# Nine of 49 blocks of a graph layer summed from gathered rows instead of packed slots

## The chip, the cores and the metric

The kernel runs on one core of one Trainium2 chip. The metric is the device time of one execution in microseconds, as the median of several runs; the profile is of one more execution and gives the span from the core's first to its last instruction. Five engines work side by side, each through its own fixed list of instructions: TensorE (PE, with weight loads as PEld), VectorE (DVE), ScalarE (ACT), GpSimd (POOL) and the sync engine (SP), whose list here holds DMA issues. An instruction may wait for semaphores; everything behind it in the same list then waits too.

## What is computed

One relational graph layer with a residual and a layer norm, on 6,250 nodes of 128 features and 100,000 edges that are sorted by destination:

```python
Xs = X[src]
m_data = Xs @ W_data.T + b_data
m_ctrl = Xs @ W_control.T + b_control
msg = jnp.where((edge_types == 0)[:, None], m_data, m_ctrl)
agg = jax.ops.segment_sum(msg, dst, num_segments=X.shape[0])
out = jax.nn.relu(agg + (X @ W_self.T + b_self))
x = layernorm(x + out)
```

Every edge takes the row of its source node under one of two linear maps and adds it to its destination node. All of it is float32; the kernel carries each float32 value as three bfloat16 parts that sum to it, which is why rows have 384 columns.

## The kernel before

**Lead-in (0 to about 100 us).** `load_x` and `split_x` bring x in, transposed, in seven parts and split it in three bfloat16 parts (`x3`). `multiply` forms both linear maps for all 49 blocks of 128 nodes (49 x 2 = 98 sub-tables, `NT`) with nine matmuls a block and a bias matmul; `take` and `leave` split the results in three parts again. They stay in SBUF as `m3`, and `store` also writes them to a table in DRAM. `store_x` writes the split x to DRAM (`x3_t`).

**Edges.** The destinations are cut into 49 blocks of 128 nodes. Since edges are sorted, the edges of a block lie in one window of 2,304 edges (`WIN`, 18 rows of 128, `KT`). `starts` finds where each window begins and loads it.

**Packing (per group of five blocks, `GROUPS`).** The rows of `m3` are already on the chip, so a block's messages are not fetched one by one. For each block, the up to 32 edges (`R`) of each of the 98 sub-tables get slots: `bucket_hots` and `ranks` (matmuls into `acc`, reductions into `slot`) number the edges of each sub-table, `fill_a` and `fill_b` (matmuls into `small`) put the source row and the destination of each slot into place, `fill_c` writes the slots to DRAM (`packed`) and handles edges that found no slot: it fetches up to 32 such rows with an indirect DMA from the table (`msg_s`).

**The main loop (per block).** `spread` reads the block's slots back to all partitions (`rows`, 784 KB), `select` makes them one-hot on VectorE. Then 25 tiles (`NS`) follow. A tile covers four sub-tables of 32 slots: `gather` multiplies four one-hots of 32 columns by the rows of `m3` into a PSUM tile `g_ps`, `evict` copies it to SBUF as `gs` on ScalarE, and `add_up` multiplies it by the one-hot of destinations (`hot_d`) into `agg`, in four column matmuls. `own_of` adds the node's own map (12 matmuls on x read from `x3_t`, `load_own`), and the last tile adds the leftover rows and the bias. `finish_blocks` and `normalise` do the rest on VectorE and ScalarE, and the result is stored a group at a time.

**The order.** All these are generators whose steps name a cost by engine, the steps they need and a due time. A planner (`Order.run`) places the steps while the kernel is built: among those that can start within `CLOSE` of the earliest it takes the one due first. The result is a fixed order on each engine. `BLOCK` is the planned time of a block, `BUILT` the planned end of the lead-in. When the program runs, only semaphores hold the engines to each other.

**Buffers.** PSUM has eight banks: three of `ps_a` (`small`, `acc`, `agg`; one each) and five of `ps_g` (`GB`). `row_pool` holds `RB` blocks of rows, `EB` = 8 tiles of `gs`.

Of the kernel before, what the change touches and what calls it, by code (L numbers as in the profile page):

```python
# [19 lines left out]
P = 128  # L20
# [12 lines left out]

GROUPS = (4,) + (5,) * 9
Q = max(GROUPS)
NPG = len(GROUPS)
STARTS = [sum(GROUPS[:i]) for i in range(NPG)]
R = 32
NS = (NT + 3) // 4
NC = 4 * NS  # L40
RB = 4
M = 8
SLOT = 128.0
PARTS = (4, 8, 8, 8, 8, 8, 5)
KC = 6
DC = 13
# [3 lines left out]
class Order:  # L50
# [9 lines left out]
    AFTER = 0.25  # L60
    CLOSE = 0.2

# [38 lines left out]
def kernel(  # L101
# [24 lines left out]


    nc = tc.nc
    dram = ctx.enter_context(tc.tile_pool(name="dram", bufs=1, space=DRAM))
    const = ctx.enter_context(tc.tile_pool(name="const", bufs=1))  # L130
    table = dram.tile([NT * P, D3], BF16, name="table")
    x3_t = dram.tile([NB, D, 3 * P], BF16, name="x3_t")
    packed = dram.tile([NB, NT * R], BF16, name="packed")
    total = const.tile([1, 1], I32, name="total")
# [69 lines left out]
def sums_over_windows(ctx, tc, x, xt, edges, w, bias, table, x3_t, packed, total,  # L204
# [3 lines left out]
    const = ctx.enter_context(tc.tile_pool(name="consts", bufs=1))  # L208
    work = ctx.enter_context(tc.tile_pool(name="work", bufs=2))
    row_pool = ctx.enter_context(tc.tile_pool(name="row_pool", bufs=RB))  # L210
    ps_a = ctx.enter_context(tc.tile_pool(name="ps_a", bufs=1, space=PSUM))
# [30 lines left out]
    counted = {}  # L242
    for n in sorted({DC, *GROUPS}):
        counted[n] = const.tile([P, P, n], BF16, name=f"count{n}")
        G.iota(counted[n], pattern=[[1, P], [0, n]], base=0, channel_multiplier=0,
               allow_small_or_imprecise_dtypes=True)
# [34 lines left out]
    def three_parts(parts, whole, left):  # L281
# [17 lines left out]
    spill_tiles = [(const.tile([P, Q * P], BF16, name=f"hot_s{i}"),  # L299
                    const.tile([P, D3], BF16, name=f"msg_s{i}")) for i in range(2)]  # L300
    slot_values = [const.tile([P, (Q + 1) // 2, NC], BF16, name=f"vs{i}") for i in range(2)]
    slot_b = {n: const.tile([P, R, n], BF16, name=f"slot{n}") for n in sorted({*GROUPS})}

    def constants():
# [23 lines left out]

        for hot, msg in spill_tiles:
            V.memset(hot, 0.0)  # L330
            V.memset(hot[R : R + 1, :], 1.0)
            V.memset(msg, 0.0)
            V.tensor_copy(msg[R : R + 1, :].rearrange("p (i c) -> p i c", i=3),
                          parts[0:1, :, 2 * D :])

    win = {}
    first = const.tile([1, NB], I32, name="first")
    counts = const.tile([P, NPG], F32, name="counts")
    m3 = const.tile([P, NT, D3], BF16, name="m3")
    m3v = m3.rearrange("p (t b) c -> p t b c", t=2)  # L340

    def starts():
# [12 lines left out]
        V.tensor_scalar_min(first, first_ps[:1, :NB], float(E - WIN))  # L355
        for b in range(NB):
            grp = [g for g in range(NPG) if STARTS[g] <= b][-1]
            yield step(("win", b), {"S": 0.84}, "first", *([("fields", grp - 2)] if grp > 1 else []),
                       lag=2.0)
            if b == STARTS[grp]:  # L360
                win[grp] = work.tile([P, Q, KT, 3], I32, name="win")
            at = nc.values_load(
                first[0:1, b : b + 1], engines=(SP,), min_val=0, max_val=E - WIN,
                skip_runtime_bounds_check_because="it counts edges and is held to E - WIN",
            )
            nc.sync.dma_start(
                win[grp][:, b - STARTS[grp], :, :],
                edges[ds(at, WIN), :].rearrange("(p k) c -> p k c", p=P),
            )
# [8 lines left out]
    LEAD, BUILT = 12.0, 85  # L378
    BLOCK = 13.5
    AHEAD = 12.0  # L380

    def due(kind, *i):
        if kind in ("p", "g") and i[0] in ("root", "rooted", "scale", "apply", "out"):
            n = i[1] + 1
            return BUILT + 10 + BLOCK * sum(GROUPS[:n])
        if kind in ("counted", "turned", "first"):
# [13 lines left out]
        if kind in ("win", "xs", "agg", "o", "whole", "sum"):  # L400
            b = i[0]
            begun = BUILT + BLOCK * b
            if kind == "win":
                return begun - 2 * BLOCK * GROUPS[1] - 20
            return begun + {"whole": BLOCK + 0.5, "sum": BLOCK + 3}.get(kind, 0.3 * BLOCK)
        if kind in ("rows", "sel", "d", "g", "e", "s"):
            of = {"rows": 1, "sel": 1, "d": 2}.get(kind, NS)
            lead = {"rows": -9, "sel": -3, "d": -1, "g": 0, "e": 1, "s": 2}[kind]
            return BUILT + BLOCK * (i[0] + (i[1] / of if len(i) > 1 else 0)) + lead
        n = GROUPS[i[0]]  # L410
        end = BUILT + BLOCK * STARTS[i[0]] - AHEAD
# [14 lines left out]
    def load_x():  # L426
        for g, n in enumerate(PARTS):
            yield step(("xt", g), {"A": 0.45}, *([("x3", g - 3)] if g > 2 else []), lag=4.0)
            xts[g] = build.tile([D, max(PARTS), P], F32, name="xt", bufs=3)[:, :n]
            A.dma_start(xts[g].rearrange("p b c -> p (b c)"),  # L430
                        xt[:, at_part[g] * P : (at_part[g] + n) * P])
# [21 lines left out]
    def multiply():  # L453
        for i, (g, b, n) in enumerate(two_blocks):
            free = [("yl", two_blocks[i - YB][1])] if i >= YB else ["biased"]
            yield step(("y", b), {"T": 1.08 * n}, ("x3", g), *free)
            ys[b] = y = ps_y.tile([P, 2, 2 * D], F32, name="y")
            for j in range(n):
                for i in range(3):
                    for k in range(3):  # L460
                        T.matmul(y[:, j, :], x3s[g][:, b + j - at_part[g], i, :],  # L461
                                 w3[:, k, : 2 * D], start=i == j == k == 0, stop=False,
                                 skip_group_check=True)
                T.matmul(y[:, j, :], ones_b, bias3, start=False, stop=True, skip_group_check=True)  # L464

# [242 lines left out]
    d_hots, g_tiles, gs_tiles, aggs, xss, x3b, hs_, mvs = {}, {}, {}, {}, {}, {}, {}, {}  # L708
    XS = 4
    DB, EB, GB = 4, 8, 5  # L710

# [9 lines left out]
    def select():  # L721

        for b in range(NB):
            yield step(("sel", b), {"V": 1.2}, ("rows", b))
            V.tensor_scalar(rows[b], rows[b], pid1, None, op0=ALU.is_equal)  # L725

    def to_hots():
        tiles = [(b, c) for b in range(NB) for c in range(-(-NS // DC))]
        for i, (b, c) in enumerate(tiles):
# [12 lines left out]

    tiles = [(b, g) for b in range(NB) for g in range(NS)]

# [10 lines left out]
    def evict():  # L755
        for i, (b, g) in enumerate(tiles):
            free = [("s", *tiles[i - EB])] if i >= EB else []
            e = yield step(("e", b, g), {"A": 0.37}, ("g", b, g), *free)
            gs_tiles[b, g] = gs = late.tile([P, D3], BF16, name="gs", bufs=EB)
# [15 lines left out]

    def load_own(name, blocks):
        for i, b in enumerate(blocks):
            free = [("sum", blocks[i - XS])] if i >= XS else []
            yield step(("xs", b), {"S": 0.9}, ("rows", b), "built", *free, lag=4.0)
            x3b[b] = late.tile([D, 3, P], BF16, name=f"x3_{name}", bufs=XS)  # L780
            nc.sync.dma_start(x3b[b].rearrange("p i c -> p (i c)"), x3_t[b])
            xss[b] = load_rows(b, late, f"xs_{name}", XS)

    def own_of(blocks, begun):

        for i, b in enumerate(blocks):
            yield step(("agg", b), {"S": 0.0}, *([("whole", blocks[i - 1])] if i else []))
            yield step(("o", b), {"T": 0.5}, ("xs", b), begun(b))
            for i in range(3):
                by_columns(aggs[b].rearrange("p (i c) -> p i c", i=3), x3b[b][:, i, :],  # L790
                           w3[:, :, 2 * D :], start=False, stop=False, skip_group_check=True)

    def finish_blocks():
        for b, (grp, q) in enumerate(blocks):
# [3 lines left out]
            if q == 0:  # L798
                hs_[grp] = late.tile([P, Q, D], F32, name="h_p")
                mvs[grp] = work.tile([P, Q, 2], F32, name="mv_p")  # L800
# [16 lines left out]


    late = ps_g = None

    def close_build():
        nonlocal late, ps_g
        yield step("built", {"S": 0.0}, "stores", ("yl", NB - 1), *[("x3_t", g) for g in range(len(PARTS))])
        early.close()
# [9 lines left out]
        take(1, "ym", "y1"), leave(1, "y2", "ym"), take(2, "yl", "y2"), constants(), store_x(), store(), close_build(),  # L834
        load_own("p", list(range(NB))), own_of(list(range(NB)), lambda b: ("s", b, 0)),
    ], due)


    total_ps = ps_a.tile([P, 512], F32, name="small")
    T.matmul(total_ps[:1, :NPG], ones[:, 0:1], counts, start=True, stop=True)  # L840
    total_f = work.tile([1, 1], F32, name="total_f")
    V.tensor_reduce(total_f, total_ps[:1, :NPG], axis=AX.X, op=ALU.add)
    V.tensor_copy(total, total_f)
# [121 lines left out]
```

## Time and profile before

| what | value |
|---|---|
| median of 3 runs | 721.98 us (721.96 to 722.43) |
| span of the profiled execution | 717.1 us, mean granted TensorE clock 0.990 |
| matmuls | 14,698 |
| evictions `gs` on ScalarE | 1,225, 489.5 us busy |
| indirect DMAs on GpSimd | 11 |
| bytes moved by DMA | 73.05 MB, 102 GB/s over the span |

Busy shares tell how long an engine had something in hand. TensorE's matmuls overlap: each is listed with its whole duration, while four column matmuls run beside each other, so a busy count near 100% tells that there were no pauses and not what a matmul costs; that is read from the starts of successive matmuls in the timeline. In a waits or timeline line, the bracket names how long the engine was idle before the instruction and who released it. GpSimd is almost unused: it makes some constants at the start and issues the indirect DMAs.

### The profile page before, as it was taken

What the parts mean: (1) busy time and instruction counts of PE and PEld (TensorE: products, weight loads), DVE (VectorE), ACT (ScalarE), POOL (GpSimd) and SP (SyncE); (2) the same over time, 40 slices, a digit from 0 to 9 for tenths busy, and PEclk for the clock granted to TensorE, in tenths of its full rate; (3) what the DMA queues carried; (4) which work ended last, traced back from release to release, by engine and by line L of the source; (5) the groups of instructions that cost most, each with busy time, mean ns of one, the idle gap of its engine ahead of it and who ended that gap; (6) DMA issues with size and microseconds to landing.
All of it is one profiled execution on the core that took longest, in us unless ns stands there. A gap on an engine that the chain in (4) does not pass through costs nothing.

```text
span 717.1 us, 33878 instructions
## 1 busy us (share of the span) xinstructions
PE 667.4 (93%) x14698; PEld 574.3 (80%) x14698; DVE 527.5 (74%) x1101; ACT 572.6 (80%) x1407; POOL 23.3 (3%) x21
## 2 busy tenths in 40 slices
PE   3799979999999999999989989999999999999993
PEld 2667747898898888889878888998988897887882
DVE  8565568788869958886985888699689778657321
ACT  3666546889789887888978888898889888798994
POOL 4000000000000000000000000000000000001000
PEclk9999989999999999999999999999999999999997
DMA  5566564053006105301710530160062026006200
GB/s 162 163 209 217 165 212 155 9 170 124 11 15 243 52 3 193 108 8 45 222 42 4 202 97 9 42 235 24 4 222 76 4 92 201 7 4 222 75 4 23
DMA packets 57564, 73.05 MB, mean 102 GB/s; under 512 B 12292, under 2 KB 50191, under 8 KB 57359
## 3 DMA queue, kind: packets, MB, share of 16 engines
q1 hardware_dynamic: 55806, 66.70, 28.6%
q10 hardware_dynamic: 1154, 3.41, 1.5%
q8 instruction: 116, 1.90, 1.1%
q0 software_dynamic: 448, 0.72, 0.3%
q14 instruction: 40, 0.33, 0.2%
HBM read 52.85 MB, written 17.96 MB: 99 GB/s over the span
## 4 chain that ended last, share of the span: by engine, by line
PE 57%; DVE 24%; DMA 10%; ACT 3%; issue 3%; SPq 1%; DVEq 0%; ACTq 0%
PE agg L220 21%; PE g_ps L752 17%; PE acc L220 7%; PE small L603 5%; DVE slot L565 4%; DMA x_p<-x_t 4%; DMA out<-h_p 4%; PE y L461 4%; DVE hot_d L739 4%; DVE hot_st L548 3%; DVE two L586 3%; ACT h_p L179 2%; DVE rows L725 1%; DVE hr L581 1%; PE y L480 1%
## 5 line engine op out<-in xcount | busy, mean ns | idle before, releaser
L760 ACT CAST gs<-g_ps 128x384 bf16<-128x384 f32 x1225 | 489.5, 514 | 67.9 <-PE g_ps L752 61.5
L220 PE MATMUL agg<-gs,hot_d 128*32 128x384 bf16 x4900 | 407.1, 332 | 2.8 <-ACT gs L760 1.9
L752 PE MATMUL g_ps<-m,rows 128*32 128x384 bf16 x4900 | 399.9, 328 | 3.1 <-DVE rows L725 2.8
L220 PEld LDWEIGHTS <-hot_d 128*32 128x32 bf16 x4900 | 232.5, 137 | 28.4 <-issue 5.9
L752 PEld LDWEIGHTS <-rows 128*32 128x32 bf16 x4900 | 217.0, 137 | 22.6 <-issue 5.6
L565 DVE TENSOR_REDUCE slot<-acc 128x5 bf16<-128x490 f32 (+1 forms) x180 | 117.5, 653 | 78.7 <-PE acc L220 76.1
L739 DVE TENSOR_TENSOR hot_d<-count,to 128x1664 bf16<-128x1664 bf16 x98 | 104.6, 1068 | 11.4 <-PE agg L220 9.1
L220 PE MATMUL acc<-hot_st,rest 128*32 128x490 bf16 (+1 forms) x680 | 72.8, 375 | 13.7 <-DVE slot L565 13.2
L220 PE MATMUL acc<-hot_st,tri 128*32 128x490 bf16 (+1 forms) x720 | 77.7, 370 | 1.3 <-DVE hot_st L548 1.3
L548 DVE TENSOR_TENSOR hot_st<-count,st_b 128x2940 bf16<-128x2940 bf16 (+1 forms) x30 | 58.8, 1964 | 16.0 <-PE small L603 8.1
L473 ACT CAST m<-y 128x512 bf16<-128x512 f32 (+1 forms) x75 | 40.5, 580 | 31.7 <-PE y L464 23.8
L603 PE MATMUL small<-hot_st,two 128*32 128x98 bf16 x1764 | 64.9, 291 | 0.0
L461 PE MATMUL y<-w,x 128*128 128x256 bf16 x441 | 57.8, 279 | 6.1 <-DVE w L283 3.2
L603 PEld LDWEIGHTS <-two 128*32 128x32 bf16 x1764 | 60.4, 118 | 0.9 <-issue 0.2
L220 PEld LDWEIGHTS <-rest 128*32 128x32 bf16 x680 | 30.5, 96 | 34.1 <-issue 30.3
L461 PEld LDWEIGHTS <-x 128*128 128x128 bf16 x441 | 43.7, 100 | 13.3 <-issue 3.2
L725 DVE TENSOR_SCALAR rows<-rows,pid 128x3136 bf16<-128x3136 bf16 x49 | 50.2, 1024 | 4.0 <-DMA rows<-packed 3.9
L142 DVE TENSOR_REDUCE whole<-agg 128x128 f32<-128x384 f32 x49 | 27.1, 553 | 34.6 <-PE agg L220 33.3
L220 PE MATMUL agg<-w,x_p 128*32 128x384 bf16 x588 | 36.4, 327 | 4.0 <-DMA x_p<-x_t 3.6
L693 POOL DMA_INDIRECT msg_s<-table,row_i x10 | 14.7, 1475 | 630.1 <-PE g_ps L752 484.6
L220 PEld LDWEIGHTS <-x_p 128*32 128x32 bf16 x588 | 20.7, 97 | 9.2 <-DMA x_p<-x_t 5.4
L220 PEld LDWEIGHTS <-tri 128*32 128x32 bf16 x720 | 24.5, 97 | 2.8 <-issue 2.1
(123 smaller groups left out, 369.5 us busy)
## 6 DMA issues: line engine op xcount, KB each, us to landing
rows<-packed SPq DMA_DIRECT2D x49, 784.0 KB, 6.7
table<-m SPq DMA_DIRECT2D x10, 768.0 KB, 4.2
x_p<-x_t SPq DMA_DIRECT2D x49, 96.0 KB, 7.1
x_t<-x SPq DMA_DIRECT2D x5, 768.0 KB, 7.7
xs_p<-in_x SPq DMA_DIRECT2D x49, 64.0 KB, 6.5
xt<-in_xt ACTq DMA_DIRECT2D x5, 512.0 KB, 4.4
out<-h_p SPq DMA_DIRECT2D x8, 320.0 KB, 3.9
win<-in_edges SPq DMA_DIRECT2D x49, 27.0 KB, 1.9
```

The source lines that it names most:

```text
L142: nc.vector.tensor_reduce(whole, agg.rearrange("p (i c) -> p c i", i=3), axis=AX.X, op=ALU.add)
L220: T.matmul(out[c : c + 32], lhsT[:, c : c + 32], rhs, **flags)
L461: T.matmul(y[:, j, :], x3s[g][:, b + j - at_part[g], i, :], w3[:, k, : 2 * D], start=i == j == k == 0, stop=False, skip_group_check=True)
L473: A.copy(part_of(b, n, i), ys[b][:, :n, :].rearrange("p b (t c) -> p t b c", t=2))
L548: V.tensor_tensor(hot, counted[n][:, None, 1 : NT + 1, :].to_broadcast([P, KC, NT, n]), fields[grp][2][:, c * KC : c * KC + KC, None, :].t ...
L565: V.tensor_reduce(slots[grp][:, k, :], by_q, axis=AX.X, op=ALU.max)
L586: V.tensor_tensor(two[:, :, i], hr, f[:, ks, None, :].to_broadcast(wide), op=ALU.mult)
L603: T.matmul(vt[c0 : c0 + R, q // 2, :], two[:, k, i, :, q], hot[:, k, :, q], start=c == k == 0 and q < 2, stop=c * KC + k == KT - 1, skip_g ...
L725: V.tensor_scalar(rows[b], rows[b], pid1, None, op0=ALU.is_equal)
L739: V.tensor_tensor(hot, counted[DC][:, :, :n], places[grp][:, q, None, c * DC : c * DC + n].to_broadcast([P, P, n]), op=ALU.is_equal)
L752: T.matmul(g_ps[t * R : (t + 1) * R, :D3], rows[b][:, :, s], m3[:, s, :], start=True, stop=True)
L760: (A.copy if e == "A" else V.tensor_copy)(gs, g_tiles.pop((b, g))[:, :D3])
```

## The change

Nine of the 49 blocks are taken out of the packing. Their edges' rows are fetched directly: GpSimd issues one indirect DMA for each of the 18 rows of 128 edges of a window, 162 in all, each of which brings 128 rows of 384 bfloat16 (768 bytes) from the table in DRAM to 128 partitions. A one-hot of destinations (`hot_g`, VectorE, six of them in one instruction) then sums them with four column matmuls. No slots, no gather matmuls and no eviction are needed for these blocks. It is meant to hand work from TensorE, ScalarE and VectorE to the idle GpSimd and to the DMA queues. The 40 other blocks stay packed in eight groups of five. The gathered blocks get due times that spread them over the whole run (`PACE` = 3.2 us for each gather), so that a gathered quad of matmuls comes up between packed ones all the time.

The other parts:
- The own x of a block is loaded as soon as its part of `x3_t` is stored, into a pool of its own that exists from the start (before: only once the lead-in's buffers were closed).
- In `multiply` the bias matmuls of a pair of blocks stand behind both blocks' products, and the step waits for `bias` and no longer for `biased`.
- In the last packed group the planner may give evictions to VectorE; in the built order it gives it 15 of 125.
- To make room: four `g_ps` tiles (`GB`) instead of five, three blocks of rows (`RB`) instead of four, two `xt` buffers instead of three. The gathered sums take a PSUM bank of their own (`agg_g`), the gathered rows three buffers (`MB`), their one-hots two (`XB`).
- `BLOCK` 13.5 to 13.2, `CLOSE` 0.2 to 0.1. The windows of the nine blocks are loaded right behind those of the first two groups.

```diff
-GROUPS = (4,) + (5,) * 9
+GROUPS = (5,) * 8
...
-RB = 4
+XS = 4
+RB = 3
...
-    CLOSE = 0.2
+    CLOSE = 0.1
...
+    hot_b = const.tile([P, P], BF16, name="hot_b")
+    msg_b = const.tile([P, D3], BF16, name="msg_b")
...
-        for b in range(NB):
-            grp = [g for g in range(NPG) if STARTS[g] <= b][-1]
+        for b in [*range(STARTS[2]), *range(NPB, NB), *range(STARTS[2], NPB)]:
+            grp = [g for g in range(NPG) if STARTS[g] <= b][-1] if b < NPB else NPG
...
-    BLOCK = 13.5
+    BLOCK = 13.2
+    PACE = 3.2
...
+        if kind in ("gh", "gm", "msg"):
+            k = i[1] * CH if kind == "gh" else i[1]
+            return BUILT + PACE * (i[0] * KT + k) + {"msg": 0, "gh": 2, "gm": 5}[kind]
...
-            xts[g] = build.tile([D, max(PARTS), P], F32, name="xt", bufs=3)[:, :n]
+            xts[g] = build.tile([D, max(PARTS), P], F32, name="xt")[:, :n]
...
-            free = [("yl", two_blocks[i - YB][1])] if i >= YB else ["biased"]
+            free = [("yl", two_blocks[i - YB][1])] if i >= YB else ["bias"]
...
+            for j in range(n):
                 T.matmul(y[:, j, :], ones_b, bias3, start=False, stop=True, skip_group_check=True)
...
-    DB, EB, GB = 4, 8, 5
+    DB, EB, GB = 4, 8, 4
...
-            e = yield step(("e", b, g), {"A": 0.37}, ("g", b, g), *free)
+            costs = {"A": 0.37, "V": 0.53} if b >= STARTS[-1] else {"A": 0.37}
+            e = yield step(("e", b, g), costs, ("g", b, g), *free)
...
-            yield step(("xs", b), {"S": 0.9}, ("rows", b), "built", *free, lag=4.0)
+            yield step(("xs", b), {"S": 0.9}, ("x3_t", part), *free, lag=4.0)
...
+    def gather_rows():
+        for i, (j, k) in enumerate(gathered):
+            free = [("gm", *gathered[i - MB])] if i >= MB else [*stored, "built", "idx"]
+            yield step(("msg", j, k), {"G": PACE}, *free, lag=3.0 - PACE)
+            msgs[j, k] = late.tile([P, D3], BF16, name="msg", bufs=MB)
+            G.indirect_dma_start(
+                out=msgs[j, k], out_offset=None, in_=table[:, :],
+                in_offset=bass.IndirectOffsetOnAxis(ap=idx[:, j, k : k + 1], axis=0),
+            )
...
+    def gathered_sums():
+        for j, k in gathered:
+            free = [("agg", NPB + j)] if k == 0 else [("o", NPB + j)] if k == KT - 1 else []
+            yield step(("gm", j, k), {"T": 0.165}, ("msg", j, k), ("gh", j, k // CH), *free)
+            if k == 0:
+                aggs[NPB + j] = ps_a.tile([P, D3], F32, name="agg_g")
+            by_columns(aggs[NPB + j], g_hots[j, k // CH][:, :, k % CH], msgs.pop((j, k)),
+                       start=k == 0, stop=k == KT - 1, skip_group_check=True)
```

## The prediction

> **What bounds the kernel now.** I read the page's busy shares first, then a table of busy time by stage, then TensorE's timeline, GpSimd's timeline and the DMA landings.
>
> ```profile
> PE 667.4 (93%) x14698; PEld 574.3 (80%) x14698; DVE 527.5 (74%) x1101; ACT 572.6 (80%) x1407; POOL 23.3 (3%) x21
> ...
> core 0: us, PE busy (x) PEld busy (x) DVE busy (x) ACT busy (x) POOL busy (x), PEclk, DMA share, GB/s
> 95.00:126.00 31.00, 25.48 (x488) 17.85 (x489) 23.60 (x60) 17.15 (x43) 0.87 (x1) 0.89 0.64 212
> 438.00:498.00 60.00, 59.19 (x1428) 52.74 (x1424) 49.68 (x105) 52.27 (x133) 1.70 (x1) 1.00 0.26 90
> 650.00:705.00 55.00, 53.44 (x1148) 43.22 (x1144) 21.98 (x50) 53.58 (x140) 2.77 (x1) 1.00 0.25 86
> ```
>
> From about 106 to 650 us TensorE is busy nearly all the time (59.2 of 60 us); ScalarE and VectorE have slack (52 and 50), GpSimd does nothing. From 650 on, with no more buckets to fill, ScalarE is full instead (53.6 of 55). Busy counts overlapping matmuls, so I take TensorE's real price from the timeline:
>
> ```profile
> 115.60 0.34 PE L752 MATMUL g_ps<-m,rows 128*32 128x384 bf16 x4
> 115.76 0.34 PE L220 MATMUL agg<-gs,hot_d 128*32 128x384 bf16 x4
> 115.92 0.34 PE L752 MATMUL g_ps<-m,rows 128*32 128x384 bf16 x4
> ...
> 676.07 1.21 PE L752 MATMUL g_ps<-m,rows 128*32 128x384 bf16 x20
> ...
> 685.83 1.22 PE L752 MATMUL g_ps<-m,rows 128*32 128x384 bf16 x20
> ```
>
> Columns: start, duration, what. Four column matmuls start every 0.162 us though each lasts 0.34: 0.0405 us apiece. The same mark recurs 9.76 us later in the last blocks; that is 25 evictions at 0.39 us, ScalarE's pace.
>
> The new load falls on GpSimd, so I read its few indirect DMAs (32 rows each, the first 49) and the landings:
>
> ```profile
> 8.34 1.13 POOL L275 DMA_INDIRECT er<-in_edges,row_i  x1 [0.20 <-issue]
> ...
> 218.01 1.70 POOL L693 DMA_INDIRECT msg_s<-table,row_i  x1 [61.23 <-PE g_ps L752]
> 278.66 0.87 POOL L693 DMA_INDIRECT msg_s<-table,row_i  x1 [58.95 <-PE g_ps L752]
> ...
> 651.58 2.77 POOL L693 DMA_INDIRECT msg_s<-table,row_i  x1 [61.27 <-PE g_ps L752]
> ...
> 218.58 1.01 DVE L725 TENSOR_SCALAR rows<-rows,pid 128x3136 bf16<-128x3136 bf16 x1
> ...
> rows<-packed SPq DMA_DIRECT2D x49, 784.0 KB, 6.7
> ...
> msg_s<-table,row_i POOLq DMA_INDIRECT x10, 6.5
> ```
>
> The undisturbed one takes 0.87 us. The one at 218.01 meets the selection of rows on VectorE (218.58 to 219.59) and ends at 219.71, just after it. Landing is 6.5 us at the median, 2.7 at the least.
>
> **What the skill says.** (1) "SBUF — State Buffer", section "Who interferes with whom": GpSimd and VectorE share a port pair under an exclusive lock; a VectorE instruction in a two-port mode, or with two SBUF inputs against a GpSimd read, blocks the other fully. The trace agrees: 0.87 becomes 1.70 and 2.77. (2) "DMA: Bandwidth & Descriptors", section "Anatomy of one DMA — SWDGE (gpsimd) path": generation is "small, variable", and the fixed cost of some 2 us is completion. Ten gathers of 32 rows and one of 49 cannot show the slope up to 128. (3) "TensorEngine Tiling (Array Packing)", section "PSUM Bottleneck": after a tiled TensorE the PSUM copy may bound, so both ScalarE and VectorE should evict. The window 650 to 705 shows it.
>
> **The change, part by part.**
>
> *TensorE.* Nine blocks fewer packed: 9 x 200 = 1,800 gather and sum matmuls x 0.0405 = 72.9 us. Two groups of ranks fewer (program order: 1,400 down to 1,120 matmuls into acc, four per 0.21 us): 280 x 0.052 = 14.6. Bucket matmuls 1,764 to 1,440, at 64.9 us / 1,764 = 0.037: 12.0. Small ones, about 1. Added: 9 x 18 x 4 = 648 matmuls on gathered rows x 0.0405 = 26.2. The own-feature and bias matmuls of a gathered block (12 and 4) equal the 12 and 4 it had. Net -74.3.
>
> *ScalarE and VectorE.* ScalarE loses 225 evictions (489.5 / 1,225 = 0.40 each), 90 us. VectorE loses 9 selections, 18 one-hots, 36 slot reductions, 6 bucket one-hots and their fills (1.02, 1.07, 0.65, 1.96, 2.1): about 76 us; it gains 27 one-hots of 768 elements (by size, 768/1,664 x 1.07 = 0.5) and 15 evictions (bounded by the PSUM reduction of the same 384 columns, 0.55): 22 us. Both stay under TensorE, so this is worth nothing by itself until the tail.
>
> *Tail.* ScalarE keeps 110 of the last 125 evictions: 8.6 us a block instead of 9.76. TensorE needs 216 x 0.0405 = 8.75 for the block plus about three gathered quads, 9.3, and now binds. The quads' 0.5 us were counted above, so -(9.76 + 0.5 - 9.3) x 5 = -5.
>
> *Lead-in.* The own matmuls of block 0 waited 1.6 us for x at 113 to 115 us; the early load removes that. But the first gathered quad stands some 4 us of TensorE work behind the first block's first tile (105.8 us before), and its gather may go only when the last table stores (issued at 101.3) have landed, so about 108; in the burst of row broadcasts there it lands 6.5 later. All packed matmuls stand behind that quad: about 5 us in place of 1.6, +3. Bias matmuls last and the wait for the bias hide in TensorE's lead-in, which runs on without a gap from 50 us: 0. Extra loads of edge windows on the DMA queue: 0, before TensorE's queue drains.
>
> *The new wait.* A gathered quad is in TensorE's fixed order; if its message is late, everything behind it stops, then ScalarE and VectorE. Three message buffers: gather k waits for quad k-3. In the built order 73 matmuls lie between quads, and by the prices above 9.1 us of TensorE work lie from quad k-3 to quad k (8.1 at the fifth percentile). In that time GpSimd must issue and the data land. GpSimd's time for 128 rows is not in the trace. Lower end: 0.87, were rows free. Slope from 32 to 49 rows: (1.13 - 0.87)/17 = 15 ns a row, hence 0.87 + 96 x 0.015 = 2.4. Upper end: proportional, 4 x 0.87 = 3.5. I take up to 2.4, as the 49-row one also ran beside VectorE, plus 0.45 for the lock: the VectorE work that blocked it, or has two inputs of that kind, fills about 40% of the time (hot_d 104.6, hot_st 58.8, rows 50.2 and the fills some 63 us of 717), and a meeting cost 0.83 to 1.9. Together 2.9. That is under the 3.2 us at which the quads come (9.1 / 3 and stalls). Landing was 6.5 in bursts with the 32-row issue included; with 2 us more, about 8.5 against 9.1. So it holds, barely, in bursts (DMA share 0.26 of the time): I charge +8, from 0 to 40.
>
> *End.* The last four quads close TensorE's order back to back and the very last gather waits for the fourth from last: issue 2.4 and landing some 1.5: +4. Four PSUM tiles instead of five for gather results, three row buffers instead of four: at most a few us, taken as +2.
>
> Sum: 717.1 - 74.3 - 5 + 3 + 8 + 4 + 2 = 654.8 of span. The metric stands 4.9 above the span (722.0 against 717.1), which gives 659.7. From the other side: a steady group costs 61.5 us, with 1.125 gathered blocks of (72 + 16) x 0.0405 = 3.6 it costs 65.5, so 13.1 a packed block: 106 us of lead-in, 35 x 13.1, 5 x 9.3, and 25 for the slow start (95 to 126 has 5.5 us idle and a lower clock) and the last outputs: 636 of span, 641. I take 653, above the middle of 641 and 660, since stalls have a floor and no ceiling.
>
> **Rivals.**
> A: *Messages come late.* In bursts the loop of three buffers needs 0.2 + 2.9 + 7.5 = 10.6 us per three quads instead of 9.7; over all 54 rounds 572 us, from 108 to 680, and 20 for end and metric: 700. For it: 6.5 us landings for a quarter of the size. Against: only about a quarter to a third of the run has the queues full.
> B: *GpSimd becomes the bound and the kernel is slower.* At 3.5 us proportional and 0.45 for the lock: 162 x 3.95 = 640; 108 + 640 + 17 = 765. The crossing with the old time lies at (722 - 125)/162 = 3.7 us a gather. For it: 2.77 us already seen for 32 rows. Against: 49 rows cost 1.13, far from proportional.
> C: *ScalarE paces it and TensorE's saving is lost.* Its load falls from 53.3 to about 54 per 65.5 us: it does not bind before the tail.
>
> **How the numbers follow.** Forecast (634 to 680): 0.65. A (680 to 720): 0.21. B: 0.12. Within 0.2%: 0.01, C included; the rest lies below 634. Faster is forecast, low rest and A: 0.87. The range begins at 634 (the 641, with some of the 68 us that TensorE's 649 us of pure work leaves idle now closed by the quads) and reaches to 712, which takes in most of A and leaves B out: some 0.83 in all.
>
> **What would show it.** Right: the 162 indirect DMAs of 128 rows average under 3.2 us on GpSimd; TensorE at 9 tenths in all middle slices; its idle time before the gathered quads under 20 us in total; 13.1 us a packed block; the tail at about 9.3. Wrong: GpSimd busy near 80% or more with each gather near 4 us; TensorE's idle time before quads of 50 us or more, released by DMA; the saving of matmuls there but in gaps.

## The result and the profile after

| | before | after |
|---|---|---|
| median | 721.97 us | 689.91 us (688.36 to 690.45) |
| ratio | 1 | 0.9555 (95%: 0.9536 to 0.9574) |
| span of the profiled execution | 717.1 us | 688.1 us |
| first gather matmul (`g_ps`) | 105.8 us | 122.1 us |
| mean time of a packed block, middle of the run | 12.3 us | 14.1 us |
| same, near the end (mean of three) | 9.9 us | 10.4 us |

The kernel became 32 us faster where 69 were forecast. The rows on the first `g_ps` and on the mean block tell where the rest stayed: the main loop begins 16 us later, and each of its packed blocks takes 1.0 us more than the 13.1 that the forecast gave it.

The busy shares of after, and three stretches of it (the columns are those shown of before; the last stretch is the last packed group):

```profile
PE 615.4 (89%) x12874; PEld 527.2 (77%) x12874; DVE 490.4 (71%) x1021; ACT 478.5 (70%) x1140; POOL 213.8 (31%) x181
```

```profile
95.00:126.00 31.00, 24.13 (x310) 16.43 (x311) 16.98 (x39) 12.54 (x28) 2.38 (x2) 0.85 0.61 214
438.00:498.00 60.00, 58.43 (x1370) 52.22 (x1365) 49.04 (x114) 48.45 (x121) 21.46 (x19) 1.00 0.37 113
612.00:676.00 64.00, 57.32 (x1280) 50.41 (x1276) 46.68 (x106) 44.34 (x107) 20.33 (x19) 1.00 0.31 92
```

TensorE still counts as busy for 58.4 of 60 us in the middle stretch. But it starts 1,370 matmuls there where it started 1,428 before: a matmul is listed with 0.33 us and the next starts after 0.04, so pauses of up to 0.3 us don't show in the busy count, and a count near 100% does not tell that there were none. ScalarE has fallen from 52.3 to 48.5 us, and in the last group, where ScalarE was full before, it is busy 44 us of 64. GpSimd is at a third. So no engine's work alone is the bound, and the table of waits is the next view. Two lines of before, then three of after (engine, line and tile that waited, for whom, us in total, times, longest):

```profile
ACT gs L760 <- PE g_ps L752: 61.5, 71, 5.2
...
PE acc L220 <- DVE slot L565: 13.2, 18, 2.7
```

```profile
ACT gs L780 <- PE g_ps L771: 86.9, 153, 3.0
...
DVE far_g L853 <- DMA win<-in_edges: 6.2, 1, 6.2
...
PE agg_g L228 <- DMA msg<-table,idx: 5.0, 5, 2.6
```

ScalarE waits for TensorE twice as often as before, though it has 262 evictions fewer. The quads wait for messages only five times. And the gathers are cheap, as the view of the tile `msg` says (count, shortest, median and longest in ns):

```profile
L866 POOL DMA_INDIRECT msg<-table,idx x162: 943/949/2672, 124.5 to 673.4; - x162
```

128 rows take 0.95 us of GpSimd where 32 took 0.87; the mean is 1.16.

I also add up TensorE's pauses from the starts of its matmuls: what lies between two starts beyond 0.0405 us (0.051 for `acc`, 0.0365 for `small`). In the middle of the run that is, on balance (starts that come early count against it), 25 us of 495 before and 53 us of 482 after. By place, with the early starts left out, 52 us stand ahead of `g_ps` and of sums of evicted tiles (17 before), the two ends of the hand-over to ScalarE; ahead of `acc`, the ranks, it is some 7 us where it was 24 before. So the hand-over lost more than the totals say, and another wait grew shorter.

### The profile page after: what moved, and what is told of

It reads as the page before. It is cut to its first block, busy times and chain, and to the rows that moved or that the text cites. A ratio compares the mean times of both kernels' runs of the same rounds, so it can differ in the third digit from the quotient of the medians.

```text
span 688.1 us, 29925 instructions
## 1 busy us (share of the span) xinstructions
PE 615.4 (89%) x12874; PEld 527.2 (77%) x12874; DVE 490.4 (71%) x1021; ACT 478.5 (70%) x1140; POOL 213.8 (31%) x181
## 4 chain that ended last, share of the span: by engine, by line
PE 77%; DMA 7%; DVE 5%; ACT 5%; issue 2%; SPq 1%; ACTq 0%; another core or an unknown queue 0%
PE agg L228 26%; PE g_ps L771 23%; PE acc L228 8%; PE small L623 7%; PE y L480 6%; PE agg_g L228 5%; ACT gs L780 4%; DMA rows<-packed 3%; DMA msg<-table,idx 3%; PE y L500 1%; DVE slot L585 1%; ACT h_p L186 1%; PE y L484 1%; DMA packed<-vs 1%; DMA win<-in_edges 0%
## 5 line engine op out<-in xcount | busy, mean ns | idle before, releaser
L780 ACT CAST gs<-g_ps 128x384 bf16<-128x384 f32 x963 | 397.6, 498 | 128.8 <-PE g_ps L771 86.9
L771 PE MATMUL g_ps<-m,rows 128*32 128x384 bf16 x4000 | 353.6, 331 | 14.1 <-ACT gs L780 8.2
L228 PE MATMUL agg<-gs,hot_d 128*32 128x384 bf16 x4000 | 346.1, 333 | 13.0 <-ACT gs L780 9.5
L866 POOL DMA_INDIRECT msg<-table,idx x162 | 188.4, 1163 | 321.6 <-PE agg_g L228 154.4
L585 DVE TENSOR_REDUCE slot<-acc 128x5 bf16<-128x490 f32 x144 | 95.4, 662 | 87.3 <-PE acc L228 56.5
L228 PE MATMUL agg_g<-msg,hot_g 128*32 128x384 bf16 x648 | 68.5, 330 | 5.3 <-DMA msg<-table,idx 5.0
L228 PE MATMUL acc<-hot_st,rest 128*32 128x490 bf16 x544 | 61.2, 377 | 9.0 <-DVE slot L585 8.4
L228 PE MATMUL acc<-hot_st,tri 128*32 128x490 bf16 x576 | 64.4, 374 | 0.0
L480 PE MATMUL y<-w,x 128*128 128x256 bf16 x441 | 58.4, 289 | 3.6 <-DVE x L464 1.1
L568 DVE TENSOR_TENSOR hot_st<-count,st_b 128x2940 bf16<-128x2940 bf16 x24 | 47.7, 1992 | 12.9 <-PE small L623 11.6
L713 POOL DMA_INDIRECT msg_s<-table,row_i x8 | 14.1, 1760 | 136.8 <-DVE counts L723 109.8
L228 PEld LDWEIGHTS <-hot_g 128*32 128x32 bf16 x648 | 32.1, 124 | 7.9 <-issue 6.3
```

Source lines behind the costliest of these rows:

```text
L228: T.matmul(out[c : c + 32], lhsT[:, c : c + 32], rhs, **flags)
L480: T.matmul(y[:, j, :], x3s[g][:, b + j - at_part[g], i, :], w3[:, k, : 2 * D], start=i == j == k == 0, stop=False, skip_group_check=True)
L568: V.tensor_tensor(hot, counted[n][:, None, 1 : NT + 1, :].to_broadcast([P, KC, NT, n]), fields[grp][2][:, c * KC : c * KC + KC, None, :].t ...
L585: V.tensor_reduce(slots[grp][:, k, :], by_q, axis=AX.X, op=ALU.max)
L771: T.matmul(g_ps[t * R : (t + 1) * R, :D3], rows[b][:, :, s], m3[:, s, :], start=True, stop=True)
L780: (A.copy if e == "A" else V.tensor_copy)(gs, g_tiles.pop((b, g))[:, :D3])
```

## The experiments

All ratios are against the kernel before, run beside them on the same chip. By ratio, the kernel after stands at 0.9555, and at 0.9616 when it was run again on another chip; only the last experiment was run beside it, so a difference to it of under some 4 us is not resolved. The first four runs shared one chip, the next eight a second, the four of "how many blocks" and the combinations a third, the last two a fourth; the chip of the first result is not on record.

**The lead-in: who delays the first gather matmul?** In after, VectorE does two tiny instructions for 9 us while GpSimd writes the constant `count` three times (the first fence is VectorE's timeline, the second GpSimd's: start, duration, what):

```profile
1.94 8.99 DVE L262 TENSOR_SCALAR slot_f<-iota_f 128x32 f32<-128x32 f32 x1
2.30 8.70 DVE L268 TENSOR_SCALAR ident<-iota_f,pid 128x128 f32<-128x128 f32 x1
```

```profile
1.77 9.13 POOL L253 IOTA count<- 128x640 bf16 x3
```

Before, `slot_f` took 1.07 us: it got in between the first and the second of three iotas that took 6.38 us together. (The tables repeat each number 4, 5 and 13 times before, and 5, 6 and 13 times after.) Then, from 52 to 58 us, VectorE stands for the windows of the nine blocks, and TensorE stands for 4.3 us, from 57 to 61, for what VectorE had behind that:

```profile
57.98 0.27 DVE L853 TENSOR_SCALAR far_g<-win_g 128x162 int32<-128x162 int32 x1 [6.16 <-DMA win<-in_edges]
```

```profile
61.34 0.39 PE L228 MATMUL acc<-hot_st,rest 128*32 128x490 bf16 x4 [4.26 <-DVE slot L585]
```

Two edits, one for each:

```diff
-        G.iota(counted[n], pattern=[[1, P], [0, n]], base=0, channel_multiplier=0,
-               allow_small_or_imprecise_dtypes=True)
+        A.copy(counted[n], iota_f[:, :P, None].to_broadcast([P, P, n]))
...
-            yield step(("win", b), {"S": 0.84}, "first", *free, lag=2.0)
+            yield step(("win", b), {"S": 0.84}, "first", *free, lag=2.0 if b < NPB else 26.0)
```

> The changed kernel with the three constant tables of counts copied by ScalarE from the first iota instead of made by three iotas on GpSimd. Theory L (the iotas hold the SBUF port that GpSimd and VectorE share: two small VectorE instructions stand for 9 us behind them and start the lead-in 4 us later than before): VectorE's first instructions each take under 1 us, the split of w begins at about 5 us instead of 12, the first gather matmul comes at 115 to 118 instead of 122 us, time 683 to 687 us. Rival (the lead-in has slack elsewhere: the waits for windows and for the packing of group 0 end it): the start moves, the first gather matmul stays at 121 to 122, time 688 to 691 us.

Measured: 683.05 us, ratio 0.948 (0.9449 to 0.951); first `g_ps` at 115.4 us.

> The changed kernel with a planned landing of 26 us instead of 2 for the windows of the nine gathered blocks, so that the step that turns them into row numbers stands later in VectorE's order. Theory W (VectorE stood 6.2 us behind the landing of these windows at 52 to 58 us, and TensorE 4.3 us behind VectorE): the pause of 4.3 us at 57 to 61 us goes, the first gather matmul comes 4 us sooner, time 685 to 687 us. Rival (the pause only moves, to another wait of the lead-in): 689 to 691 us.

Measured: 683.85 us, ratio 0.9504 (0.9468 to 0.954); first `g_ps` at 115.9. Each takes away 6 to 7 us of start, and about as much of time (by ratio 4 to 5). With the counts on ScalarE the same instruction of VectorE is short (its timeline), and the split of the weights, which begins at 5.5 us before and at 12.0 in after, begins at 4.5. So some 6 of its 7 us are what the change had lost; the rest the kernel before lost too.

```profile
1.95 0.16 DVE L261 TENSOR_SCALAR slot_f<-iota_f 128x32 f32<-128x32 f32 x1
```

Both edits together:

> The kernel after with both repairs of the lead-in: the counts are copied by ScalarE instead of written by three iotas on GpSimd, and the chain for the gathered blocks' fields is placed 26 us, not 2 us, after their edge windows were asked for. If the two losses are separate (6.9 and 6.1 us alone), about 677 us and TensorE's first matmul on rows near 109 us. If both only open the same gap, 682 us, first matmul near 115 us.

Measured: 680.47 us, ratio 0.9431 (0.9405 to 0.9457); first `g_ps` at 108.7. The start moves by all of 13.4 us, the time by only 9: the later stage gives some back (its pauses are 57 us instead of 53). The kernel then starts within 3 us of before, and is still far from the forecast.

**PSUM tiles, row buffers and settings.** One tile fewer for `g_ps` (`GB`): four instead of five in the kernel before, three instead of four in after.

> The kernel before with four PSUM tiles for gather results instead of five, nothing else. Theory 1 (the fifth tile, given up for the bank of the gathered sums, is what the change lost in the main loop: TensorE's waits before g_ps and agg matmuls rose from 17 to 52 us there): slower than before by 20 to 35 us, 742 to 757 us, and TensorE's pauses at the gather and sum matmuls rise above 40 us between 126 and 621 us. Theory 2 (the gathered quads and their late messages disturb the order; four tiles are enough): within 5 us of before, 717 to 727 us.

> The changed kernel with three PSUM tiles instead of four, the suspected cost taken once more. Theory 1 (too few PSUM tiles between TensorE and ScalarE): much slower, 725 us or more (over 35 us lost). Theory 2 (quads and messages): within 10 us of 690.

Measured: 728.81 us, ratio 1.0122 (1.0088 to 1.0156), and 699.31 us, ratio 0.9706 (0.9676 to 0.9737). Before falls between the ranges of the two theories, after at the edge of the second. A tile is worth about 9 us, more than the "at most a few us" of the forecast and less than a main cause. Then the settings: `CLOSE` back to 0.2 in after, and all three settings of the change (`RB` 3, `CLOSE` 0.1, `BLOCK` 13.2) in before.

> The kernel after with the closeness setting of the order back at 0.2 (0.1 in the change, 0.2 before). Theory O (the order that the new setting gives is a cause of the main stage's stalls): 5 us or more faster or slower than the kernel after's 690. Theory P (PSUM tiles and bursts at a change of group): within 3 us of it, 687 to 693.

> The kernel before with the change's settings alone: three row buffers instead of four, closeness 0.1 instead of 0.2, 13.2 instead of 13.5 us planned for a block. Theory O (row buffers and order cost the change what it lost in its main stage): 730 us or more, +10 or more over before. Theory P: within 4 us of before, 718 to 726.

Measured: 686.18 us, ratio 0.951 (0.9486 to 0.9534), so a few us faster than after at most; and 709.71 us, ratio 0.9843 (0.9819 to 0.9866), 12 us faster than before. The second falls on the side that neither theory named. Its waits show what the settings do for the kernel before: 13.2 us in which `acc` matmuls waited for `slot` became 3.0.

```profile
PE acc L220 <- DVE slot L565: 3.0, 6, 0.9
```

So tile and settings, each measured alone in the kernel before, about cancel (+9, -12), and neither explains the pauses of after. The three settings were not taken apart.

**The gathers themselves.** `gather_rows` keeps its steps and thereby the order, but issues nothing; the quads multiply a constant tile.

```diff
-            msgs[j, k] = late.tile([P, D3], BF16, name="msg", bufs=MB)
-            G.indirect_dma_start(
-...
+            msgs[j, k] = msg_b
```

> The kernel after, its order of instructions kept, but the 162 gathers of 128 rows are not issued and the gathered sums multiply a constant message tile (so the nine gathered blocks come out wrong; TensorE's work is the same). Theory G (the gathers, their traffic and what is queued behind them on GpSimd cause the extra stalls of the main stage, above all the spilled rows' gather that waits behind them): 15 to 25 us off the kernel after, about 665 to 675 us, and TensorE's stall in 130 to 612 us falls from 53 to under 35 us. Theory P (the tighter PSUM rotation and the bursts of work on VectorE and ScalarE at a change of group cause them, whatever the messages do): at most 6 us off, that is the 5 us in which gathered quads waited, 684 to 690 us, stalls still near 50 us.

Measured: 644.02 us, ratio 0.8929 (0.8903 to 0.8955): 46 us less, more than either theory named, where the waits for messages were 5. TensorE's list is the same but for the tile, its pauses fall from 53 to 16 us, a packed block takes 12.9 us and one near the end 9.6. ScalarE's line on the page (busy, mean ns, idle before, and what ended most of it) shows the idle time going, with evictions as long as before:

```profile
L780 ACT CAST gs<-g_ps 128x384 bf16<-128x384 f32 x963 | 394.6, 498 | 84.4 <-PE g_ps L771 51.6
```

In after the same line ends in 128.8 and 86.9. The frequent instructions of ScalarE and VectorE last as long in both traces (medians equal to 0.02 us); only what lies between them differs. So I measured the hand-over: of the evictions that ScalarE stood idle for, how long after the start of the last matmul of their quad do they start? Worked out from the starts in the traces, middle of the run:

| kernel | evictions with ScalarE idle | median us | later than 0.6 us |
|---|---|---|---|
| before | 123 | 0.43 | 6 |
| after | 196 | 0.72 | 116 |
| no gathers | 147 | 0.43 | 10 |

In after, 113 of the 116 fall beside a gather on GpSimd, and 69 of them begin 0.3 to 0.6 us after that gather's end, as if the quad had only then ended; some 100 of the 162 gathers have such an eviction. The trace also records TensorE's semaphore updates. Around 101 undisturbed gathers of 0.95 us, counted from their start, there are 13 updates in the stretch from 0.6 to 1.2 us, and 278 in the next 0.4 us; VectorE's are as frequent in the first stretch as before it (54 against 67). By these records TensorE's signals are held back for some 0.6 us and then come in a heap. Theory S is made of that, and four runs test it. First the same bytes without GpSimd:

```diff
-            G.indirect_dma_start(
-...
+            nc.sync.dma_start(msgs[j, k], table[k * P : (k + 1) * P, :])
```

> The kernel after, but each of the 162 messages of 128 x 384 is loaded by a plain DMA of the same size from SyncE's queue (fixed rows of the table, so the gathered blocks' values are not the reference's); buffers, waits and TensorE's order stay. Theory S (while GpSimd writes a gather's descriptors, TensorE's signals to the other engines are held back, so an eviction starts up to 0.7 us late and TensorE then waits for it): about 645 to 655 us, and evictions that ScalarE stands idle for start 0.43 us after the last matmul of their quad, as with no gathers at all. Theory T (the messages' traffic and landing, whoever issues them, delay the other transfers and the quads): 680 to 690 us.

Measured: 683.42 us, ratio 0.9494 (0.9464 to 0.9524). The time lies in the range of theory T and misses that of theory S; the hand-over meets theory S: 24 of 163 idle-before evictions are late, and their lateness beyond 0.45 us sums to 7 us against 79 in after. The pauses ahead of `g_ps` and sums are halved, 26 us. What came in their place is a new wait, for messages that stand in SyncE's one list, most of the long ones behind the 784 KB rows:

```profile
PE agg_g L228 <- DMA msg<-table: 33.6, 20, 7.8
```

Then the suspected cost alone, in the kernel before: 162 gathers into a tile `got` that nobody reads, of 128 rows and of 32.

```diff
+    def extra():
+        for i in range(162):
+            needs = [("extra", i - 1)] if i else [*stored, "built"]
+            yield step(("extra", i), {"G": 3.2}, *needs)
+            got = late.tile([P, D3], BF16, name="got")
+            G.indirect_dma_start(out=got[:128], out_offset=None, in_=table[:, :],
+                in_offset=bass.IndirectOffsetOnAxis(ap=any_i[:128, 0:1], axis=0))
```

> The kernel before with 162 gathers of 128 table rows added on GpSimd, one after the other as each lands, into a tile that nobody reads. Theory S: 46 us / 162 = 0.28 us each, so 722 + 46 = about 765 us (750 to 775). Theory M (what costs is that TensorE's quads wait for messages): nothing waits here, so 718 to 728 us. Theory T: slower as well, in proportion to the bytes (see the next run).

> The same with 32 rows instead of 128 in each of the 162 added gathers: a quarter of the bytes, but 0.87 against 0.95 us of GpSimd's time each. Theory S: nearly the same loss as with 128 rows, 745 to 770 us. Theory T: a quarter of the loss, 728 to 736 us if 128 rows give 765.

Measured: 760.82 us, ratio 1.0573 (1.0539 to 1.0607), and 746.49 us, ratio 1.0361 (1.0325 to 1.0398). Late evictions: 104 of 179 and 105 of 180. The tile's lines (the first of 128 rows, the second of 32):

```profile
L717 POOL DMA_INDIRECT got<-table,any_i x162: 940/947/2752, 116.6 to 717.9; - x162
```

```profile
L717 POOL DMA_INDIRECT got<-table,any_i x162: 866/872/2282, 116.3 to 703.4; - x162
```

Nothing waits for these gathers, and they cost 41 and 27 us. A quarter of the rows keeps two thirds of the loss and all of the late evictions: that part goes with the number of gathers. The other third goes with the rows; whether by their bytes or otherwise was not tested.

**A hand-over with more slack.** A tile's sum is placed behind the next tile's eviction:

```diff
-            ... ("e", b, g), ("d", b, g // DC), *free)
+            ... ("e", *tiles[min(i + 1, len(tiles) - 1)]), ("d", b, g // DC), *free)
```

> The kernel after with the order changed in one rule: a tile's sum stands behind the next tile's eviction, so that a tile has one eviction more of time between its gather matmuls and its sum. Theory S (late signals for evictions, 0.3 us lost at each gather because the hand-over has no slack): the stalls fall by about half, 660 to 675 us. Theory T: the transfers are as before, 683 us or more.

Measured: 680.15 us, ratio 0.945 (0.942 to 0.948). The signals are as late (107 evictions), the pauses fall from 53 to 41 us, a quarter and not half, and the time lies between the ranges of the two theories. The pauses ahead of `g_ps` stay (some 27 us, 25 in after), those ahead of the sums fall from 28 to 17: a tile of PSUM still has to come free within four tiles. With the lead-in's repairs, and then with `CLOSE` 0.2 and six message buffers besides:

> The kernel after with the two repairs of the lead-in (counts copied by ScalarE, the gathered blocks' fields later) and the sum one eviction later. The repairs act in different stages, so if they add up: 690 - 9 - 10 = about 671 us (668 to 674). If the later sum only moved time that the lead-in's repairs also give back, 677 us or more.

> The same with the closeness setting at 0.2 and six message buffers instead of three. Theory S (the signals during a gather are what is left): four us from the setting, at most five from messages that are never late, 661 to 669 us, and evictions that ScalarE stands idle for are as late as before. Theory M (late messages after all): 655 us or less.

Measured: 640.35 us, ratio 0.8914 (0.8878 to 0.8949), and 636.26 us, ratio 0.8854 (0.8826 to 0.8882). The first is some 30 us faster than forecast. The second lies under theory S by 25, in the range of theory M ("late messages after all"), but not for its reason: with six buffers the quads wait for messages about 1 us in the middle of the run, and with three, at 640, they waited 8 us in the whole run. What is gone in both is the late evictions (6 of 159 and 4 of 153). They ran on another chip than all runs so far, so the kernel after and the combination were run once more, together:

> The kernel after, unchanged. If the late signals belong to the chip: on a chip with them 688 to 692 us, on one without them about 690 - 35 = 655 us (645 to 662), with evictions 0.43 us after their quads. If they belong to the kernel: 688 to 692 us and late signals on any chip.

> The combination of the three repairs, unchanged. If the late signals belong to the chip: on a chip with them 668 to 674 us with some 100 late evictions, on one without them 638 to 643 us. If they belong to the kernel: 638 to 643 us and no late evictions on any chip.

Measured, on a fourth chip: 692.19 us, ratio 0.9616 (0.9583 to 0.965), 114 of 193 late; and 665.79 us, ratio 0.9249 (0.9219 to 0.9278), 111 of 201 late. The late signals do not belong to the kernel: they go with the chip, or with something else that differed between the two sessions, since each of these two chips was used once, and the kernel after never ran on the chip without them. The granted clock is not it: from 200 to 500 us it is 1.00 in both. The kernel before, with its eleven gathers, does not notice, 719 to 722 us on all of them; the combination differs by 25 us. The semaphore records agree: around the gathers of under 1 us, TensorE's updates from 0.6 to 1.2 us after the start number 124 (of 89 gathers) on the chip without late signals and 10 (of 93) on the other, in the same kernel. Here is one place of it, the same gather and the same quads, on both. The chip with late signals first (the timelines of TensorE, ScalarE and GpSimd, in this order):

```profile
228.51 0.39 PE L770 MATMUL g_ps<-m,rows 128*32 128x384 bf16 x4
228.68 0.39 PE L228 MATMUL agg<-gs,hot_d 128*32 128x384 bf16 x4
228.84 0.39 PE L770 MATMUL g_ps<-m,rows 128*32 128x384 bf16 x4
...
229.65 0.44 PE L228 MATMUL acc<-hot_st,tri 128*32 128x490 bf16 x4
230.24 0.39 PE L228 MATMUL agg<-gs,hot_d 128*32 128x384 bf16 x4 [0.15 <-ACT gs L779]
```

```profile
227.92 1.28 ACT L779 CAST gs<-g_ps 128x384 bf16<-128x384 f32 x3
229.71 1.24 ACT L779 CAST gs<-g_ps 128x384 bf16<-128x384 f32 x3 [0.51 <-PE g_ps L770]
```

```profile
228.33 0.95 POOL L865 DMA_INDIRECT msg<-table,idx  x1 [1.96 <-PE agg_g L228]
```

And the one without:

```profile
221.61 0.35 PE L770 MATMUL g_ps<-m,rows 128*32 128x384 bf16 x4
...
222.75 0.39 PE L228 MATMUL acc<-hot_st,tri 128*32 128x490 bf16 x4
222.95 0.35 PE L228 MATMUL agg<-gs,hot_d 128*32 128x384 bf16 x4
```

```profile
221.09 2.60 ACT L779 CAST gs<-g_ps 128x384 bf16<-128x384 f32 x6
```

```profile
221.38 0.94 POOL L865 DMA_INDIRECT msg<-table,idx  x1 [1.75 <-PE agg_g L228]
```

The quad that starts at 228.51 is evicted at 229.71, 0.43 us after the gather ended at 229.28; ScalarE had been idle for half a microsecond, and TensorE, which needs that tile, starts its sum 0.59 us after the `acc` matmuls ahead of it. On the other chip the same quad (221.61) is evicted on time in an unbroken row of six, and the sum follows after 0.20 us.

**How many blocks to gather?** 35 packed and 14 gathered, and 45 and 4, in place of 40 and 9, on the chip without late signals (`PACE` 2.2 and 7.5, the rest as in the run with six message buffers):

> The kernel of the run before with 35 blocks packed and 14 gathered (252 gathers) in place of 40 and 9 (162). By the prices of the forecast a gathered block saves TensorE 100.5/9 - 26.2/9 = 8.3 us. Theory S (each gather costs 0.28 us besides, 5.1 us a block): 3.2 us a block, so 16 us less (10 to 22). If a gather costs nothing once its message comes in time: 41 us less.

> The same with 45 blocks packed and 4 gathered (72 gathers). Theory S: 16 us more than with nine (10 to 22). If a gather costs nothing once its message comes in time: 41 us more.

Measured: 636.64 us, ratio 0.8844 (0.8813 to 0.8874), beside 636.26 with nine; and 702.73 us, ratio 0.9757 (0.9717 to 0.9797). Both miss both theories. With four, the 41 us of TensorE's prices come, and TensorE's pauses are 41 us against 19 besides. With 14, the last gather matmul of a packed block starts at 567.9 us, but 44 quads are left, and each then waits for its own message at 1.2 to 1.3 us a gather (TensorE's timeline; the quads' own time is 0.16):

```profile
615.21 0.53 PE L228 MATMUL agg_g<-msg,hot_g 128*32 128x384 bf16 x4 [0.75 <-DMA msg<-table,idx]
616.51 0.53 PE L228 MATMUL agg_g<-msg,hot_g 128*32 128x384 bf16 x4 [0.77 <-DMA msg<-table,idx]
617.75 0.53 PE L228 MATMUL agg_g<-msg,hot_g 128*32 128x384 bf16 x4 [0.71 <-DMA msg<-table,idx]
```

The planned pace put them too late: 252 gathers at 2.2 us end long after 35 blocks at 13.2. An order that ends both kinds of blocks together, and 14 blocks on a chip with late signals, were not tried.

## Why the prediction was right or wrong

*TensorE's prices: right.* Without gathers a packed block takes 12.9 us (forecast 13.1) and one near the end 9.6 (9.3); on the chip without late signals the combination takes 13.2. The saving in work was there, and the direction with it.

*ScalarE, VectorE and rival C: right.* Neither became a bound.

*GpSimd's time and rival B: on the safe side.* 2.9 us a gather were taken, 1.16 came, of which the lock can have at most some 0.2 (the mean less the median of 0.95) where 0.45 were taken. The slope per row was read from one gather that ran beside VectorE (and gives 2.3 rather than 2.4); 32 and 128 rows differ by 0.08 us.

*The new wait: this step failed.* It asked whether the message comes in time, and charged 8 us; that came to 5, of which 2.6 are the very last quad's. It put what else a gather does, while GpSimd runs it, at nothing. The runs show that TensorE's signals to ScalarE come some 0.6 us late meanwhile, on three of four chips, so that the tightest hand-over of the kernel stalls at some 100 of the 162 gathers. Size: 35 packed blocks at 14.1 us instead of 13.1 are 35 us, and the last five at 10.4 instead of 9.3 are 5. By the runs: 46 us with everything that the gathers cost, messages and bytes included; 25 us between two chips in the combination, whose order has more slack. How much of the 46 the late signals alone are is not measured for the kernel after.

*The lead-in, "+3": mis-sized, it was 16.* Two of its terms were costed at nothing or left out. "Extra loads of edge windows on the DMA queue: 0" overlooked that VectorE waits for them in its list, with the ranks of the first group behind (6 us). The `count` tables, one of them longer because six one-hots are made at a time, were not seen as a cost at all (6 us). With both put right the start is 3 us behind before, as forecast. On this the Trainium skill could have been read further: "SBUF — State Buffer", section "Who interferes with whom", says of GpSimd and a VectorE instruction in a two-port mode that whoever issues first keeps the shared port pair for the whole instruction. The forecast used the lock for the gathers, the longest of which took 2.67 us, and not for the constants at the start. That the lock held VectorE here fits the run without the iotas (0.16 us) but was not tested by itself. The trace goes beyond the page: VectorE stood not through one instruction but through three in a row, 9 us.

*Four PSUM tiles and three row buffers, "+2": mis-sized.* The tile costs 9 us. The row buffers were tried only together with `CLOSE` and `BLOCK`, and the three gave 12 in the kernel before; that the sum comes near +2 is luck.

*The tail and the end.* The last blocks are in the step above. The 4 us charged for the end were right in kind and came to about 3: the last gather starts only after the first of the closing quads, and TensorE stands for it (GpSimd's timeline, then TensorE's):

```profile
673.41 0.95 POOL L866 DMA_INDIRECT msg<-table,idx  x1 [2.69 <-PE agg_g L228]
```

```profile
672.74 0.72 PE L228 MATMUL agg_g<-msg,hot_g 128*32 128x384 bf16 x12
676.07 0.38 PE L228 MATMUL agg_g<-msg,hot_g 128*32 128x384 bf16 x4 [2.61 <-DMA msg<-table,idx]
```

From the last sum to the end of the span it is 12.0 us against 11.8 before.

*The sum from the other side.* Its 636 us of span become 636 + 16 + 35 + 5 = 692 with the three measured terms; the span was 688.

*Rival A (700 us) came nearest in number, for a cause that is not there:* its messages were to be late, and TensorE's quads waited for them five times in the run, 5 us in all.

Not settled: why the chips (or sessions) differ, and what in a gather holds TensorE's signals back. That it is GpSimd's writing of descriptors fits the trace (the delay lies within and just behind the instruction, plain DMAs from SyncE do not cause it, and it hardly depends on the number of rows), but no run looked inside. "DMA: Bandwidth & Descriptors", section "Anatomy of one DMA — SWDGE (gpsimd) path", calls that writing "small, variable"; 0.87 and 0.95 us agree with that; what it does to others is not in it.

## What to carry to other kernels

When work goes to an idle engine, ask not only whether its results come in time but what its instructions do to the hand-overs of the others: compare, in the traces, the time from a producer's last instruction to an idle consumer's start. A loop that hands tiles over every half a microsecond with little to spare loses at each disturbance: here one tile fewer cost 9 us, and a consumer placed one tile later bought some 10 back. Follow also each small constant and each early load to the instruction that waits for it in an in-order list, and measure on more than one chip before putting a price on a mechanism.

## What the runs showed of the hardware

- An indirect DMA of 128 rows of 768 bytes takes GpSimd 0.95 us, one of 32 rows 0.87 us.
- Around such a gather, from 0.6 to 1.2 us after its start, TensorE's semaphore updates are held back on three of four chips. The same kernel on two chips: 10 updates in that stretch against 124, and 111 of 201 idle-before evictions late against 6 of 159.
- Three iotas of 128 x 640, 128 x 768 and 128 x 1,664 on GpSimd kept two small float32 instructions of VectorE waiting from 2 to 11 us; the same copies took ScalarE 2.9 us, and VectorE's instruction 0.16.
